# A hand-ordered pipeline drain: scatters in pairs, a fourth expert tile, other row buffers, and the second set of sums in parts

## The chip, the cores and the metric

The kernel runs on one core of a Trainium2 chip. The metric is device time in microseconds (us), the median of several runs. Beside it there is one profiled execution, with a time of its own, from which all durations below are taken.

## The reference, cut to what matters

Two layers work on an image of 2 x 256 x 56 x 56, that is 6272 tokens of 256 channels. The first layer (a convolution with neighbourhood attention) is not touched by the change. The second layer is this, per token:

```
t = t + attn(ln(t))      # linear attention, then a feed-forward of 512 units, each with a layer norm
#   Q = elu(q)+1, K = elu(k)+1;  KV = sum over an image's tokens of K*v;  msg = Q KV / (Q . sum K)
#   msg = layernorm(msg @ Wm);  h = relu([x, msg] @ W1) @ W2;  x + layernorm(h)
t = t + ffn(ln(t))       # 8 experts of 1024 units, the two best per token
#   probs = softmax(xt @ Wr);  top 2, weights normed to 1
#   y_e = gelu(layernorm(x) @ W1[e]) @ W2[e];  out = sum of weight * y_e over the two
```

All of it is float32. The two images have separate sums KV and K, so a second image's queries need its own sums.

## The kernel before, in words

**Groups and stages.** Layer 2 works on 49 blocks of 128 tokens, in 14 groups: eleven of four blocks, two of two, and one of one block (which holds the border of both images). A group is named below by its first block and its size, (45,2) for blocks 45 and 46. A group passes four stages, one step `s` of the main loop (L1777) apart: `queries` (letter q, two parts), `message` (m, two parts), `feed_forward` (f, four parts of the first matrix, then one for each two blocks of the second) and `route` (r, two parts, then p and P in the next step). Each of them is a generator. A part ends at a `yield`.

**The order.** TensorE's instructions are issued in the order in which they are traced (`manual_schedule`), and that order is written out by hand, as strings with a letter for each part: `turns` for the steps up to 11, `last` for steps 12 to 17. These last six steps are called the drain here: the queue of groups runs out, and expert tiles fill in. The other engines are ordered by the planner from its own priorities; `tc.issue_after(ins)` forces what is traced in its block to come behind `ins` on the same engine.

**Sums.** `merged(b, ...)` turns the key sums of image b into `ksm` and `mw`, in three rounds of matmuls with an eviction behind each. Image 1's runs at the end of step 5, behind `close_keys`, in one go.

**Route.** It normalises a group's rows into `row` (L147, on VectorE), whose columns 256 to 259 are the token number (copied from `dest` on GpSimd, L1710), two weights, and the better expert's number (copied on GpSimd, L1671). It transposes the rows (`pts`, L1486), multiplies by the router's weights (`pl`, L1719), picks two experts (`top_two`, a chain of some fifteen small VectorE instructions, with an Exp on ScalarE, L1657), and, after the part p with the matmuls `pp` (L1734 and L1735) on `chosen` (L1726), knows each row's place. Part P then writes every block's rows to DRAM (`xs`) with two indirect scatters per block on GpSimd (L160), all eight of a group in one part, behind the newest power of `route` (`power`). `row` has two buffers; a group of one block leaves the rest of its buffer to the next (`spare`).

**Powers.** Every inverse root is a power on GpSimd (`rs`, L254 and L1698). GpSimd also adds the residual (`t_b`, L1639), prepares an expert tile's output (`yt`, L1341) and scatters it with accumulation into `y` (L160 again).

**Expert tiles.** `Experts.run` takes tiles of 256 rows. One tile is 32 matmul instructions `ph` (L1359, four parts) with Gelu on ScalarE behind them (L1363), then `px` (L1332), the next tile's transposes, then 32 `py` (L1377, four parts). With a first part for the first transposes, three tiles are 25 parts: the letter e. `NFI` is the number of tiles that run in the drain; the others follow in a stage of their own (1407 to 2082 us) in which nothing else uses TensorE much.

**The end.** Tokens that received their last expert output late are read back, transposed (`pto`, L1866), evicted (`o_sb`, L1871 on ScalarE and L1873 on VectorE) and written out. `o_sb` comes from the pool `p4o`, which has four buffers.

Of the kernel before, what the change touches and what calls it, by code (L numbers as in the profile page):

```python
# [12 lines left out]
F32 = mybir.dt.float32  # L13
AF = mybir.ActivationFunctionType
ALU = mybir.AluOpType
# [4 lines left out]
P = 128  # L20
B, C, HH, WW = 2, 256, 56, 56
# [35 lines left out]
NFS, NHS = 48, 5  # L57
NFI = 3
XW = C + 4
# [59 lines left out]
def hybrid_kernel(ctx: ExitStack, tc: tile.TileContext, a: dict, out: bass.AP):  # L119
# [26 lines left out]
    def norm(out_, in_, mv, rstd, i):  # L146
        nc.vector.tensor_scalar(  # L147
            out_, in_, mv[:, i, 0:1], rstd[:, i : i + 1], ALU.subtract, ALU.mult
        )
# [16 lines left out]
    evac_n = [0]  # L166
    newest = [None]

# [80 lines left out]
    def rstd(sm, var, scale):  # L249
        n = var.shape[1]  # L250
        r = sm.tile([P, 4], F32, name="rs")
        with tc.high_priority():
            nc.vector.tensor_scalar(r[:, :n], var, scale, 1e-5, ALU.mult, ALU.add)  # L253
            nc.gpsimd.tensor_tensor(r[:, :n], r[:, :n], mhalf[:, :n], ALU.pow)  # L254
        return r
# [851 lines left out]
    class Experts:  # L1107
# [235 lines left out]
        def run(self, ts, pools, between=lambda i: None):  # L1343
# [7 lines left out]
            for i, (t, nh) in enumerate(ts):  # L1351
# [22 lines left out]
                for h in range(nh):  # L1374
                    py = pools.py(h)
                    for j in range(NJ):
                        nc.tensor.matmul(  # L1377
                            py, hT[:, j, h * P : (h + 1) * P], x.w2[:, j, :],
                            start=(j == 0), stop=(j == NJ - 1),
                        )  # L1380
                        if j == 3:
                            yield
                    newest[0] = nc.vector.scalar_tensor_tensor(  # L1383
                        x.yt[:, h, :], py, x.eq[:, h : h + 1], x.yt[:, h, :], ALU.mult, ALU.add
                    ).ins
                    scatter(y2, x.idi[:, h : h + 1], x.yt[:, h, :], mine, others, compute_op=ALU.add)
                    yield


    def layer1(ctx, tk, behind=(None, None)):  # L1390
# [19 lines left out]
        with lin as ph:  # L1410
# [86 lines left out]
            def merged(b, kxs, kc):  # L1497


                ksm = [wp.tile([P, P], F32, name=f"ksm{b}{hg}") for hg in range(2)]  # L1500
                mw = wp.tile([P, 2, C], F32, name=f"mw{b}")
                for hg in range(2):
                    nc.vector.tensor_scalar(ksm[hg], m32, kc[:, hg : hg + 1], None, ALU.mult)
                pt = ps_a.tile([P, 512], F32, name="kxt", tag="a")
                for ct in range(2):
                    for hg in range(2):
                        nc.tensor.transpose(
                            pt[:, (2 * ct + hg) * P : (2 * ct + hg + 1) * P],
                            kxs[:, hg, ct * P : (ct + 1) * P], ident,
                        )  # L1510
                kxt = wk.tile([P, 512], F32, name="kxt_sb", tag="tmp", bufs=4)
                evac(kxt, pt)
                kxt = kxt.rearrange("p (ct hg d) -> p ct hg d", ct=2, hg=2)
                pv = ps_a.tile([P, 512], F32, name="kvt", tag="a")
                kvt = wk.tile([P, 2, C], F32, name="kvt_sb", tag="u")[:, :, 0:P]
                for hg in range(2):
                    for ct in range(2):
                        nc.tensor.matmul(
                            pv[:, hg * P : (hg + 1) * P], w_v[:, ct, hg * P : (hg + 1) * P],
                            kxt[:, ct, hg, :], start=(ct == 0), stop=(ct == 1),  # L1520
                        )
                    nc.vector.tensor_tensor(kvt[:, hg, :], pv[:, hg * P : (hg + 1) * P], m32, ALU.mult)
                pm = ps_a.tile([P, 512], F32, name="mwp", tag="a")
                for hg in range(2):
                    nc.tensor.matmul(
                        pm[:, hg * C : (hg + 1) * C], kvt[:, hg, :], w_m[:, hg, :], start=True, stop=True
                    )
                evac(mw.rearrange("p hg c -> p (hg c)"), pm)
                centre(mw)
                return ksm, mw  # L1530

# [4 lines left out]
            def queries(n0, n, out):  # L1536
# [13 lines left out]
                for hg in range(2):  # L1550
                    pd = ps_q.tile([P, 512], F32, name="pd", tag="q")
                    for b, c0, c1 in parts(n0, n):
                        nc.tensor.matmul(
                            pd[:, c0:c1], sums[b][0][hg], qz[:, hg, c0:c1], start=True, stop=True
                        )
                    z = wk.tile([P, 512], F32, name="z")
                    over(z[:, :w], pd[:, :w], 1e-6)
# [48 lines left out]
            def feed_forward(n0, n, m2T):  # L1606
# [13 lines left out]
                for k0 in range(0, n, 2):  # L1620
# [26 lines left out]
            def top_two(lg, scale, row, n):  # L1647
# [32 lines left out]
                return ohs  # L1680


            spare = []
            power = [None]

            def route(n0, n):
# [3 lines left out]
                with tc.high_priority():  # L1690
# [12 lines left out]
                if n == 1:  # L1703
                    spare.append(row[:, 1:])
                row = row[:, :n]
                pts = [ps_a.tile([P, 512], F32, name="pts", tag="a") for _ in range(2)]
                for k in range(n):
                    norm(row[:, k, 0:C], t[:, k, :], mv, rs, k)
                    turn(pts, k, row[:, k, 0:C])
                nc.gpsimd.tensor_copy(row[:, :n, C], dest[:, n0 : n0 + n])  # L1710

# [33 lines left out]
                yield  # L1745

                with tc.issue_after(power[0]):
                    for k in range(n):
                        for kk in range(K):
# [3 lines left out]
                            )  # L1753
                yield

            sums[0] = merged(0, tk.kxs, tk.kc)
            kx = ps_k.tile([P, 2, C], F32, name="kx", tag="kx")
# [4 lines left out]
            for hg in range(2):  # L1764
# [5 lines left out]
            qzs, m2Ts = [], []  # L1770
            turns = "quvuvuqv", "mquvmuvquv", "mqfpPufmuqfurfvrfvfv"

            last = (
                "mqfpfmqfrfPrfef", "mqefpfemqfrePferf", "mfefpefmefrePfer", "fefpefefrePfer",
                "eeeeprePer", "eeeepP",
            )
            work = iter(())  # L1777
            tiles = iter(())


            with tc.manual_schedule(engines={mybir.EngineType.PE}):
                on = {}
                for s in range(ng + 4):
                    on = {"p": on.get("r", iter(()))}
                    if s < ng:
# [10 lines left out]
                    for part in turns[min(s, 2)] if s < ng - 2 else last[s - ng + 2]:  # L1796
                        next(tiles if part == "e" else on.get(part.lower(), iter(())), None)
                        chunk(work)
                        if part == "P" and s == early1 + 3:

                            tk.xa.close()
                            ex = Experts(ctx, tk)
                            pools = SimpleNamespace(
                                xr=lambda: wk.tile([P, 2, XW], F32, name="xr", tag="xt"),
                                xe=lambda: wk.tile([P, 2, ST], F32, name="xe", tag="ks"),
# [13 lines left out]
                            )  # L1819
                        if part == "P" and s == early2 + 3:  # L1820
                            ex.remember()
                    if s == 0:
                        prepare_feed_forward()
                    if s == 5:
                        kxs = wk.tile([P, 2, C], F32, name="kxs", tag="u")
                        kc = sm.tile([P, 2], F32, name="kc")
                        close_keys(tk, ps_a, kx, acc, kxs, kc)
                        sums[1] = merged(1, kxs, kc)
                for _ in tiles:
                    pass  # L1830

        with ExitStack() as ph:
# [7 lines left out]
            pools = SimpleNamespace(  # L1840
                xr=lambda: xp.tile([P, 2, XW], F32, name="xr"),
                xe=lambda: xp.tile([P, 2, ST], F32, name="xe"),
# [123 lines left out]
```

## Time and profile before

| what | us |
|---|---|
| median of the runs (lowest, highest) | 2113.43 (2113.14, 2123.83) |
| the profiled execution's own time | 2112.3 |
| its span, first to last instruction | 2110.5 |
| TensorE busy in the span | 1945.8 (92%) |
| VectorE, ScalarE, GpSimd busy | 1028.4, 633.4, 682.4 |
| steps 12 to 17, from the first `pm` of step 12 to the last `px` | 1246.9 to 1390.8 |
| one expert tile in its own stage | 14.26 (32 `ph` 6.91, `px` 0.44, 32 `py` 6.91) |
| TensorE busy from 2050 to 2110 | 37.7 of 60 |

The chain of work that ended last goes through TensorE for most of the second layer, so an interval in which TensorE has nothing to do there is an interval of the kernel's time. The granted clock in the profile says how much of TensorE's full speed was given in a stretch.

### The profile page before, as it was taken

Reading aid. Unit: us, or ns where it says so; the run is one execution under the profiler, and the core shown is the slowest. Engines: PE = TensorE matmul, PEld = TensorE weight load, DVE = VectorE, ACT = ScalarE, POOL = GpSimd, SP = SyncE. Lnnn points to the kernel's source line nnn. Section 1 sums busy time; section 2 is a strip of 40 time slices with the busy share of each in tenths; the row PEclk is TensorE's granted clock in tenths of the full one; section 3 lists DMA queues with packets and bytes.
Section 4 is the critical chain, followed back from the end, with each engine's and each line's share of the span. In section 5 each row is a group of like instructions: output and inputs, shape, how many; then the busy total and the mean of one; then the engine's idle time right before and its main releaser. Section 6 shows DMA issues by size and latency. Waiting matters only on the chain. (4 is left out here: it accounts for less than half of the span.)

```text
span 2110.5 us, 27961 instructions
## 1 busy us (share of the span) xinstructions
PE 1945.8 (92%) x10102; PEld 1364.8 (65%) x10102; DVE 1028.4 (49%) x2615; ACT 633.4 (30%) x1258; POOL 682.4 (32%) x800
## 2 busy tenths in 40 slices
PE   5799989999988888999999999799999999999995
PEld 3454444554434555666665657688888888888885
DVE  6777868775986656455555554351111212112121
ACT  1233323332332331333323223222222222222332
POOL 4712012111003433345444444442333333233221
PEclk9999989999988998999999999899999999999997
DMA  5642422344243214000011142377666666766994
GB/s 132 155 110 69 150 76 66 95 125 113 67 120 102 38 47 124 1 18 34 33 48 46 49 138 75 94 212 218 191 194 193 199 194 187 207 190 187 289 287 145
DMA packets 189784, 264.67 MB, mean 125 GB/s; under 512 B 26294, under 2 KB 149508, under 8 KB 189390
## 3 DMA queue, kind: packets, MB, share of 16 engines
q1 hardware_dynamic: 163598, 221.96, 34.6%
q0 software_dynamic: 20576, 29.75, 7.4%
q10 hardware_dynamic: 5456, 11.00, 1.6%
q8 instruction: 84, 1.38, 0.3%
q14 instruction: 70, 0.57, 0.1%
HBM read 196.38 MB, written 70.55 MB: 126 GB/s over the span
## 5 line engine op out<-in xcount | busy, mean ns | idle before, releaser
L1359 PE MATMUL ph<-xe,w1e 128*128 128x256 f32 (+1 forms) x1696 | 363.8, 372 | 4.7 <-DVE qz L237 3.6
L1377 PE MATMUL py<-w2e,hT 128*128 128x256 f32 x1616 | 358.6, 379 | 0.0
L1363 ACT ACTIVATE hT<-ph,sv 128x256 f32<-128x256 f32 (+1 forms) x424 | 196.3, 464 | 506.3 <-PE ph L1359 503.4
L1359 PEld LDWEIGHTS ph<-xe,w1e 128*128 128x128 f32 x1696 | 312.3, 192 | 45.8 <-DVE qz L237 3.8
L1377 PEld LDWEIGHTS py<-w2e,hT 128*128 128x128 f32 x1616 | 302.6, 190 | 38.8
L534 DVE SCALAR_TENSOR_TENSOR yc<-ypad,w,yc 128x1120 f32<-128x1120 f32 x192 | 267.3, 1395 | 46.0 <-ACT yc L532 43.0
L160 POOL DMA_INDIRECT y<-yt,idi x101 | 161.1, 1595 | 224.1 <-DVE yt L1383 133.0
L521 PE MATMUL pc<-ypad,diag 128*128 128x448 f32 x432 | 176.6, 549 | 0.5 <-ACT ypad L515 0.5
L509 PE MATMUL py<-x_sb,wq 128*128 128x448 f32 (+1 forms) x384 | 156.5, 539 | 14.6 <-ACT yc L525 9.2
L570 ACT ACTIVATE p<-p 98x680 f32<-98x680 f32 (+5 forms) x120 | 111.8, 932 | 182.9 <-DVE p L565 177.1
L565 DVE TENSOR_TENSOR p<-s_ps,tab 98x340 f32<-98x340 f32 (+5 forms) x240 | 138.1, 602 | 57.8 <-PE s_ps L561 56.3
L1315 DVE CAST idi<-xr 128x2 int32<-128x2 f32 (+1 forms) x53 | 10.0, 189 | 297.6 <-DMA xr<-xs 295.8
L1383 DVE SCALAR_TENSOR_TENSOR yt<-py,eq,yt 128x256 f32<-128x256 f32 x101 | 48.8, 483 | 210.9 <-PE py L1377 210.9
L561 PE MATMUL s_ps<-qT,kT 32*98 32x170 f32 (+5 forms) x960 | 131.3, 407 | 17.8 <-DVE p L565 16.6
L561 PEld LDWEIGHTS s_ps<-qT,kT 32*98 32x98 f32 (+1 forms) x960 | 57.6, 172 | 106.2 <-DVE p L565 59.6
L521 PEld LDWEIGHTS pc<-ypad,diag 128*128 128x128 f32 x432 | 78.1, 189 | 71.7 <-issue 68.0
L498 POOL TENSOR_SCALAR diag<-ident,w 128x128 f32<-128x128 f32 x108 | 84.9, 804 | 116.3 <-PE pc L521 109.4
L509 PEld LDWEIGHTS py<-x_sb,wq 128*128 128x128 f32 x384 | 70.9, 198 | 77.9 <-issue 54.9
L1341 POOL TENSOR_SCALAR yt<-b2e,eq 128x256 f32<-128x256 f32 x101 | 47.7, 485 | 217.1 <-DMA b2e<-in_L_ffn_b 215.2
L160 POOL DMA_INDIRECT xs<-row,si x98 | 96.4, 984 | 64.3 <-DVE si L1743 31.1
L254 POOL TENSOR_TENSOR rs<-rs,mhalf 128x2 f32<-128x2 f32 (+2 forms) x89 | 66.5, 754 | 142.1 <-DVE rs L253 118.4
L1614 PE MATMUL p<-m2T,fw 128*128 128x512 f32 (+2 forms) x224 | 94.3, 544 | 0.0
(357 smaller groups left out, 2606.0 us busy)
## 6 DMA issues: line engine op xcount, KB each, us to landing
w1e<-in_L_ffn_W SPq DMA_DIRECT2D x53, 1024.0 KB
w2e<-in_L_ffn_W SPq DMA_DIRECT2D x53, 1024.0 KB
yd<-yc SPq DMA_DIRECT2D x24, 784.0 KB
ld<-yd SPq DMA_DIRECT2D x28, 448.0 KB
xr<-xs SPq DMA_DIRECT2D x48, 260.0 KB
b2e<-in_L_ffn_b SPq DMA_DIRECT2D x53, 128.0 KB
yr<-y SPq DMA_DIRECT2D x11, 512.0 KB
td<-t_i SPq DMA_DIRECT2D x24, 224.0 KB
```

The source lines that it names most:

```text
L160: ins = nc.gpsimd.indirect_dma_start(out=dst[:, :], out_offset=bass.IndirectOffsetOnAxis(ap=index, axis=0), in_=src, in_offset=None, **kw,)
L498: nc.gpsimd.tensor_scalar(diag[:, tap, :], ident, w2[:, oc, tap : tap + 1], 1.0, ALU.mult, ALU.mult)
L509: nc.tensor.matmul(py[:, :n, :], wq1[:, ct, oc * P : (oc + 1) * P], x_sb[:, ct, (q0 + g0) * WW : (q0 + g0 + n) * WW], start=(ct == 0), sto ...
L521: nc.tensor.matmul(pc, diag[:, tap, :], ypad[:, dy : dy + 8, dx : dx + WW], start=(tap == 0), stop=(tap == 8),)
L534: nc.vector.scalar_tensor_tensor(yc[:, 8:, :], src, w, yc[:, 8:, :], ALU.mult, ALU.add)
L561: nc.tensor.matmul(s_ps[:nk, j, :n].rearrange("p (i j) -> p i j", j=nj), kT[hs], q[hs], start=True, stop=True,)
L565: nc.vector.tensor_tensor(p[:nk, 2 * pr : 2 * pr + 2, :n].rearrange("p h (i j) -> p h i j", j=nj), s_ps[:nk, :, :n].rearrange("p h (i j) - ...
L570: nc.scalar.activation(p[:nk, :, :n], p[:nk, :, :n], AF.Exp)
L1359: nc.tensor.matmul(p1, x.w1[:, ct, j * P : (j + 1) * P], x.xe[:, ct, :], start=(ct == 0), stop=(ct == 1),)
L1363: nc.scalar.activation(hT[:, j, :], p1, AF.Gelu, bias=x.sv[:, 4 + j : 5 + j])
L1377: nc.tensor.matmul(py, hT[:, j, h * P : (h + 1) * P], x.w2[:, j, :], start=(j == 0), stop=(j == NJ - 1),)
L1614: nc.tensor.matmul(p1[:, :w], fw1[:, k, oc * P : (oc + 1) * P], rhs, start=(k == 0), stop=(k == 3))
```

## The change

- `NFI` goes from 3 to 4, so a fourth expert tile runs in the drain and one fewer in the stage behind it.
- The scatters of a group are one pair per part. In the late groups each pair is issued behind the newest instruction in `newest[1]`: the last traced power of `rstd` or `route`, or the last residual addition. Expert outputs in the drain are scattered behind the same (`pools.turn`).
- The strings of the drain are written anew, with 35 letters e instead of 25. The set-up of the experts is moved to a letter of its own, c.
- Groups of fewer than four blocks take their rows from the buffers of `z`, which are made slightly larger, in place of the shared `row`.
- The expert's number is reduced straight into the row, and the token numbers are copied on VectorE behind the last norm; both copies on GpSimd go.
- `merged` is a generator with three parts. Image 1's run as the letters w in step 6.
- `p4o` has ten buffers instead of four.

```diff
-NFI = 3
+NFI = 4
     def rstd(sm, var, scale):
-            nc.gpsimd.tensor_tensor(r[:, :n], r[:, :n], mhalf[:, :n], ALU.pow)
+            newest[1] = nc.gpsimd.tensor_tensor(r[:, :n], r[:, :n], mhalf[:, :n], ALU.pow).ins
     def run(self, ts, pools, between=lambda i: None):
-                    scatter(y2, x.idi[:, h : h + 1], x.yt[:, h, :], mine, others, compute_op=ALU.add)
+                    with pools.turn():
+                        scatter(y2, x.idi[:, h : h + 1], x.yt[:, h, :], mine, others, compute_op=ALU.add)
             def merged(b, kxs, kc):
                 evac(kxt, pt)
+                yield
 ...
                     nc.vector.tensor_tensor(kvt[:, hg, :], pv[:, hg * P : (hg + 1) * P], m32, ALU.mult)
+                yield
 ...
                 centre(mw)
-                return ksm, mw
+                yield
             def queries(n0, n, out):
-                    z = wk.tile([P, 512], F32, name="z")
+                    z = wk.tile([P, 2 * XW], F32, name="z", tag="z")[:, :512]
             def feed_forward(n0, n, m2T):
-                    nc.gpsimd.tensor_tensor(tt, tt, u[:, :kn, :], ALU.add)
+                    newest[1] = nc.gpsimd.tensor_tensor(tt, tt, u[:, :kn, :], ALU.add).ins
             def top_two(lg, scale, row, n):
-                    ix = sm.tile([P, 4], F32, name=f"ix{k}")[:, :n]
+                    ix = sm.tile([P, 4], F32, name="ix")[:, :n] if k else row[:, :n, C + 3]
-                    if k == 0:
-                        nc.gpsimd.tensor_copy(row[:, :n, C + 3], ix)
             def route(n0, n):
-                    power[0] = nc.gpsimd.tensor_tensor(rs2, u, mhalf[:, :n], ALU.pow).ins
+                    newest[1] = nc.gpsimd.tensor_tensor(rs2, u, mhalf[:, :n], ALU.pow).ins
-                row = spare.pop() if spare else wk.tile([P, 4, XW], F32, name="row")
+                if n == 4:
+                    row = wk.tile([P, 4, XW], F32, name="row")
+                else:
+                    row = wk.tile([P, 2, XW], F32, name="row2", tag="z")[:, :n]
-                nc.gpsimd.tensor_copy(row[:, :n, C], dest[:, n0 : n0 + n])
+                with tc.issue_after(last.ins):
+                    nc.vector.tensor_copy(row[:, :n, C], dest[:, n0 : n0 + n])
-                with tc.issue_after(power[0]):
-                    for k in range(n):
+                for k in range(n):
+                    with tc.issue_after(newest[1]) if late else nullcontext():
                         for kk in range(K):
                             scatter(
 ...
-                yield
+                    yield
-            turns = "quvuvuqv", "mquvmuvquv", "mqfpPufmuqfurfvrfvfv"
+            turns = "quvuvuqv", "mquvmuvquv", "mqfpPPPPcufmuqfurfvrfvfv", "mwqfwpPPPPfwmqfrfrff"
             last = (
-                "mqfpfmqfrfPrfef", "mqefpefmqfrePferf", "mfefpefmefrePfer", "fefpefefrePfer",
-                "eeeeprePer", "eeeepP",
+                "mqfpcfmfqrfPPfPrPfe", "mqfpfmfqePePrePfePref", "mfefpefmeferePPfePerPe",
+                "fefeepefeferePfePere", "eeeeperPePer", "eeeepP",
             )
+                    if s == 6:
+                        on["w"] = second
-                        sums[1] = merged(1, kxs, kc)
+                        second = merged(1, kxs, kc)
-            op = ph.enter_context(tc.tile_pool(name="p4o", bufs=4, reuse_waits="tile"))
+            op = ph.enter_context(tc.tile_pool(name="p4o", bufs=10, reuse_waits="tile"))
```

More of the change, by code (lines that the diff above doesn't have):

```diff
@@ L146, in norm @@
     def norm(out_, in_, mv, rstd, i):
-        nc.vector.tensor_scalar(
+        return nc.vector.tensor_scalar(
             out_, in_, mv[:, i, 0:1], rstd[:, i : i + 1], ALU.subtract, ALU.mult
@@ L166, in hybrid_kernel @@
     evac_n = [0]
-    newest = [None]
+    newest = [None, None]
     def evac(dst, src):
@@ L1501, in merged @@
                 mw = wp.tile([P, 2, C], F32, name=f"mw{b}")
+                sums[b] = ksm, mw
                 for hg in range(2):
@@ L1680, in top_two @@
                 return ohs
-            spare = []
-            power = [None]
             def route(n0, n):
@@ L1701, in route @@
                 nc.vector.tensor_tensor(rs, rs, rs2, ALU.mult)
-                row = spare.pop() if spare else wk.tile([P, 4, XW], F32, name="row")
-                if n == 1:
-                    spare.append(row[:, 1:])
-                row = row[:, :n]
+                if n == 4:
+                    row = wk.tile([P, 4, XW], F32, name="row")
+                else:
+                    row = wk.tile([P, 2, XW], F32, name="row2", tag="z")[:, :n]
                 pts = [ps_a.tile([P, 512], F32, name="pts", tag="a") for _ in range(2)]
                 for k in range(n):
-                    norm(row[:, k, 0:C], t[:, k, :], mv, rs, k)
+                    last = norm(row[:, k, 0:C], t[:, k, :], mv, rs, k)
                     turn(pts, k, row[:, k, 0:C])
-                nc.gpsimd.tensor_copy(row[:, :n, C], dest[:, n0 : n0 + n])
+                with tc.issue_after(last.ins):
+                    nc.vector.tensor_copy(row[:, :n, C], dest[:, n0 : n0 + n])
                 x2T = tk.turned(n0, n)
@@ L1753, in route @@
                             )
-                yield
-            sums[0] = merged(0, tk.kxs, tk.kc)
+                    yield
+            for _ in merged(0, tk.kxs, tk.kc):
+                pass
             kx = ps_k.tile([P, 2, C], F32, name="kx", tag="kx")
@@ L1770, in layer1 @@
             qzs, m2Ts = [], []
-            turns = "quvuvuqv", "mquvmuvquv", "mqfpPufmuqfurfvrfvfv"
+            turns = "quvuvuqv", "mquvmuvquv", "mqfpPPPPcufmuqfurfvrfvfv", "mwqfwpPPPPfwmqfrfrff"
             last = (
-                "mqfpfmqfrfPrfef", "mqefpfemqfrePferf", "mfefpefmefrePfer", "fefpefefrePfer",
-                "eeeeprePer", "eeeepP",
+                "mqfpcfmfqrfPPfPrPfe", "mqfpfmfqePePrePfePref", "mfefpefmeferePPfePerPe",
+                "fefeepefeferePfePere", "eeeeperPePer", "eeeepP",
             )
             work = iter(())
-            tiles = iter(())
+            tiles = none = iter(())
             with tc.manual_schedule(engines={mybir.EngineType.PE}):
@@ L1783, in layer1 @@
                 for s in range(ng + 4):
-                    on = {"p": on.get("r", iter(()))}
+                    on = {"p": on.get("r", none)}
+                    if s == 6:
+                        on["w"] = second
                     if s < ng:
@@ L1795, in layer1 @@
                             on["uv"[k]] = keys(tk, wk, sm, ps_a, 4, kx, acc, groups[7 + s][0] + 2 * k, 2)
-                    for part in turns[min(s, 2)] if s < ng - 2 else last[s - ng + 2]:
-                        next(tiles if part == "e" else on.get(part.lower(), iter(())), None)
+                    for part in turns[3 if s == 6 else min(s, 2)] if s < ng - 2 else last[s - ng + 2]:
+                        next(tiles if part == "e" else on.get(part.lower(), none), None)
                         chunk(work)
-                        if part == "P" and s == early1 + 3:
+                        if part == "c" and s == early1 + 3:
                             tk.xa.close()
@@ L1803, in layer1 @@
                             pools = SimpleNamespace(
+                                turn=lambda: tc.issue_after(newest[1]),
                                 xr=lambda: wk.tile([P, 2, XW], F32, name="xr", tag="xt"),
@@ L1819, in layer1 @@
                             )
-                        if part == "P" and s == early2 + 3:
+                        if part == "c" and s == early2 + 3:
                             ex.remember()
@@ L1840, in layer1 @@
             pools = SimpleNamespace(
+                turn=nullcontext,
                 xr=lambda: xp.tile([P, 2, XW], F32, name="xr"),
```

## Prediction

> **What bounds it now.** I read the page first. TensorE is busy 92% of the span and fills the expert stage from 1407 to 2082 us, so only the holes outside that stage can be had. The 40 slices show two that this change can reach: slice 26 (1319 to 1372 us, busy 7, clock 8) and slice 40, the end. The weak slices 1 to 16 belong mostly to the first layer.
>
> ```profile
> PE 1945.8 (92%) x10102; PEld 1364.8 (65%) x10102; DVE 1028.4 (49%) x2615; ACT 633.4 (30%) x1258; POOL 682.4 (32%) x800
> PE   5799989999988888999999999799999999999995
> PEclk9999989999988998999999999899999999999997
> ```
>
> Then TensorE's waits from 1247 to 1400 us, which is the drain (columns: total us, times, longest):
>
> ```profile
> PE pp L1734 <- DVE chosen L1726: 13.4, 2, 12.0
> PE ph L1359 <- DVE qz L237: 3.6, 1, 3.6
> PE pd L1553 <- DVE m2T L175: 3.2, 1, 3.2
> ```
>
> These three lines are 20.2 us; with six small waits (3.2 us together) TensorE stands still 23.4 us. The stage table by windows adds the second price, a slow clock after the hole (columns: window, length, busy us of PE, PEld, DVE, ACT, POOL, clock, DMA share, GB/s):
>
> ```profile
> 1339.40:1351.40 12.00, 0.03 (x1) 0.00 (x0) 6.90 (x35) 2.85 (x6) 6.27 (x9) 0.70 0.24 56
> 1351.40:1358.00 6.60, 6.57 (x22) 5.79 (x23) 1.26 (x11) 1.14 (x3) 3.03 (x3) 0.51 0.11 40
> 1031.00:1040.00 9.00, 5.93 (x22) 4.76 (x22) 4.39 (x13) 0.78 (x2) 1.26 (x1) 0.65 0.09 31
> ```
>
> Why the 12 us? The timeline of GpSimd and VectorE at that place:
>
> ```profile
> 1334.41 0.17 DVE L253 TENSOR_SCALAR rs<-ssf 128x2 f32<-128x2 f32 x1 [3.35 <-ACT sq L1481]
> 1335.75 0.96 POOL L160 DMA_INDIRECT xs<-row,si  x1 [0.30 <-issue]
> 1339.34 0.18 POOL L1710 COPY row<-dest 128x2 f32<-128x2 f32 x1 [2.63 <-DMA xs<-row,si]
> 1340.01 1.60 POOL L160 DMA_INDIRECT y<-yt,idi  x1 [0.48 <-issue]
> 1341.04 1.33 POOL L254 TENSOR_TENSOR rs<-rs,mhalf 128x2 f32<-128x2 f32 x1
> 1342.40 0.88 DVE L1635 SCALAR_TENSOR_TENSOR u<-py,rs,g 128x256 f32<-128x256 f32 x2 [7.82 <-POOL rs L254]
> ```
>
> A power was wanted at 1334.6. GpSimd was in the midst of eight scatters (1.26 us each with the issue), then stood 2.6 us before the token-number copy, whose row buffer was still being read by the scatters, then scattered an expert output, and began the power at 1341.04. VectorE stood behind `u` with the router's chain of (45,2) queued after it, so `chosen` came at 1351.4, while TensorE had been given only 3.7 us of other work between `pl` and `pp`.
>
> **What the Trainium skill says.** "Advanced Engine Details and Errata", Sequencer Loop: an instruction waits in its engine's queue for its semaphores; the trace agrees, `u` and all behind it stood 7.8 us. "TensorE: Matmul & The Clock Gate", What's actually happening: an idle window of about 3.4 us halves the clock; the trace agrees after the 12 us (0.51), and shows slower matmuls after 3.2 us and 1.4 us too. "ScalarE: Activation LUTs", What ACT_TABLE_LOAD costs: 1283 ns per load; the drain has nine, mean 1283 ns. "DMA: Bandwidth & Descriptors", Anatomy of one DMA — SWDGE (gpsimd) path: about 2 us fixed; here a scatter of `row` lands after 2.5 us (median).
>
> **The change, part by part.** Warm, an 8-instruction part with 256 columns takes 1.73 us, with 512 columns 3.44; these price every letter.
>
> 1. *Pairs, rows elsewhere, copies off GpSimd, more e between `pl` and `pp`.* A power now finds at most one or two pairs (2.5 us each) and an output scatter (1.9) in front, not eight scatters. (45,2) no longer shares its buffer with groups whose scatters are under way; the two buffers of `z` are free by then, as the last queries end in step 13. Between the two parts of (45,2) the string had f e f, 3.7 us; it now has e f e f e e, 4 x 1.73 + 2 x 0.87 = 8.7 us. The undisturbed chain from `pl` to `chosen` is 3.9 us for (37,4) and 5.1 for (24,1), so it is covered. Gain: the wait of 12.0 and the slow clock (pp 1.04 for 0.22, ph 3.60 for 1.73, p 1.71 for 0.89: 3.5), **15.5**.
> 2. *An f between m and q in step 12.* `pd` waited for the m2T eviction, queued in VectorE behind four norms and the index chain until 1262.2. 3.44 us of f now run first. Gain 3.2 + slow clock (2.05 for 0.87, 4.21 for 3.44: 2.0) = **5.2**.
> 3. *The first e of step 13 behind q's second part.* `ph` waited 3.6 us for a buffer of `pq`, plus 0.7 slow. Now an f runs there. But e directly follows `pd`, whose two buffers are freed by transposes that ended 0.7 us after TensorE: I take 1.0 lost. Gain **3.3**.
> 4. *(47,2) in step 16:* five e instead of four before `pp`: 8.7 us of cover, where `pl` to `chosen` took 8.4. The 1.4 wait and 1.7 slow clock go: **3.1**.
> 5. *(24,1):* 33 parts e exist for 4 tiles, and the string uses two of them after the last `pl`: 3.5 us of cover where the chain takes 5.1, against four e (6.9) before. **-2.0** with its slow clock.
> 6. *The fourth tile* is 64 matmuls and `px` in both places: 14.3 us more in the drain, 14.26 less behind it, nothing net. Its four SP loads (0.38 us to issue each), two `yt` (0.47), one `so`, two output scatters on GpSimd and eight Gelus go along. SP's y writes and the weights have room: DMA is 0.2 to 0.4 busy there, and a tile now has 20 us or more for 2.2 MB that arrive in 14 in the later stage. If that cover failed, TensorE would wait for weights.
> 7. *New waits.* The trace of before cannot show the new order of GpSimd and VectorE. Every pair is now behind a power or a residual addition, and an output scatter too; queued behind them are the next powers and `yt`, for which VectorE waits. From below 0 (the orders fit; no gain, since an order is only added), from above a second wait like the old one, 12 with its clock 15. I take two waits of one pair, **-5**.
> 8. *Copies.* 28 GpSimd copies of 0.2 us go, 14 VectorE copies of under 0.2 come, right behind the norm that already holds the buffer. Both engines are under 60% busy: 0.
> 9. *Sums in parts.* At 1034 `kvt` waits for an eviction that sits behind statistics in VectorE, and the clock falls to 0.65:
>
> ```profile
> PE kvt L1518 <- DVE kxt_sb L175: 2.7, 1, 2.7
> ```
>
> Idle 3.1 and about 2 of slow clock. The parts w now have q and f (7 us) between; the short wait between the halves of `kvt` (0.4) stays. I take **3.5** of 5.1; from below 2.
>
> 10. *Ten buffers at the end.* From 2094 us the evictions wait for output transfers:
>
> ```profile
> DVE o_sb L1873 <- DMA out<-o_sb: 3.7, 3, 1.9
> ACT o_sb L1871 <- DMA out<-o_sb: 1.9, 2, 1.0
> ```
>
> The last group writes ten `o_sb`, so none waits. VectorE's 3.7 lie on the chain that ends last; the transfers then crowd a little. **3.0**, between 1 and 4. Twelve KB more of pool shift the later pools; what they land on is done with by 1390, so 0, at worst a couple of us.
>
> Sum: 15.5 + 5.2 + 3.3 + 3.1 - 2.0 - 5 + 3.5 + 3.0 = 26.6. The profiled execution took 2112.3 us, so 2085.7; it lies 1.1 under the median shown, so 2086.8. I say **2087**.
>
> **Rivals.**
> - *GpSimd's wait only moves.* Two pairs of (41,4) still stand ahead of `u`'s power of (47,2) in step 14, 5 us, with an output scatter 7, as long as before; then only the added cover of 5 us counts. Part 1 gives 5, parts 2 to 4 half of 11.6, less 5 and 2; with 6.5 from 9 and 10 that is 10: about 2102. For it: everything hangs on one queue that is half busy (25 of 50 us). Against: the missing 2.6 us buffer wait.
> - *ScalarE becomes the wait, and it is slower.* ScalarE takes Exp in order, ahead of Gelus, and before it stood up to 7.3 us at one Exp. `ph` has two buffers, 1.73 us of slack. Were each of five routes' Exp to fall among `ph`, TensorE would lose 2 x 1.28 + w - 1.73 each, w being the wait for VectorE. My sum without new waits gains 31.6; five such losses outweigh it from w = 5.5 us. At w = 7.3, the old longest, they cost 41, and five restarts with a cold clock 2 each (part 2's): 2112.3 - 31.6 + 51, about 2131. Against: counted by letters, each `pl` of steps 13 to 15 is followed by parts of `py`, which need no Gelu.
> - *It does not do what it says.* The planner may place pairs as before, late in a bunch; then only parts 9, 10 and the letters act, with the fourth tile's extra load: 2105 to 2115.
>
> **Chances.** Half a per cent, 10.6 us, is about what can be told from no change. My forecast 0.60 (2077 to 2098), the moved wait 0.22 (2098 to 2112, two thirds of it faster), no effect 0.08, ScalarE 0.10. So faster 0.74, same 0.14, slower 0.12. The range is 2077 (nothing in part 7, upper ends of 9 and 10) to 2112, which leaves out about 0.05 below and 0.15 above.
>
> **What would show it.** Right: no wait of TensorE over 3 us in the drain; `pp` waiting under 2; the longest run of scatters without a power two pairs; no GpSimd `row` copies; `kvt` waiting under 1; no `o_sb` waiting for `out`; the drain, from the first `pm` of step 12 to the `px` behind the last `pp`, some 138 us (144 + 14 - 20), though it holds one tile more; the stage behind it 14 us shorter. Wrong: a wait of 5 us or more at `pp`, `ph` or `u`, `ph` waiting for a Gelu, or a clock under 0.9 between 1300 and 1400.

## The result and the profile after

The changed kernel takes **2087.22 us** (median of six runs, 2085.41 to 2098.08); the kernel before, beside it, 2112.61 (six runs, 2102.24 to 2123.83). The ratio is 0.9889, with a 95% interval of 0.9853 to 0.9925. The forecast was 2087, in a range from 2077 to 2112. The number came out; the steps behind it did so only in part.

The profiled execution took 2085.57 us. From its page: the span, the busy time by engine, and two rows of the 40 slices.

```profile
span 2083.8 us, 27912 instructions
PE 1931.9 (93%) x10102; PEld 1354.2 (65%) x10102; DVE 1024.8 (49%) x2629; ACT 633.0 (30%) x1258; POOL 676.2 (32%) x772
PE   5799989999988888999999998999999999999996
PEclk9999989999997998999999999999999999999998
```

Slice 26, which stood at 7 with a clock of 8, is full; slice 25 has gone from 9 to 8, for new waits that are shown below. TensorE has the same 10102 matmul instructions; GpSimd has 28 fewer, the copies. TensorE's waits in the drain of the changed kernel (engine, operation and line, what it waited for, total us, times, longest):

```profile
PE pp L1734 <- DVE chosen L1726: 3.9, 2, 2.3
PE ph L1360 <- ACT hT L1364: 2.2, 3, 1.0
PE pp L1735 <- DVE before L1731: 2.2, 1, 2.2
PE pp L1734 <- DVE oh L1672: 2.0, 1, 2.0
```

The waits of 12.0, 3.6 and 3.2 us are gone. The longest left is 2.3.

Because one profile's total can mislead, I cut every profile at the same five instructions: the first `pm` of steps 5, 7 and 12, the `px` of the 40th expert tile before the end, and the last `py`. Counting that tile from the end makes the work of "drain" equal, whatever `NFI` is. Lengths in us:

| kernel | to step 5 | 5, 6 (sums) | 7 to 11 | drain | stage | end |
|---|---|---|---|---|---|---|
| before | 988.1 | 85.8 | 173.0 | 281.6 | 553.7 | 28.4 |
| after | 984.1 | 81.0 | 173.4 | 266.4 | 554.9 | 23.9 |

The drain gives 15.2, the sums 4.8, the end 4.5. The 3.9 us ahead of step 5 are not the change's: they are there when layer 2 begins (its first `pq` starts at 801.7 before and at 797.1 after), and the first layer is the same. Over all profiles of this study the stretch to step 5 lies between 979.0 and 991.9. It alone makes totals spread by half a per cent, so the experiments below are read by their stretches first. (In the diff of the change one old string is misprinted; step 13 of the kernel before reads `mqefpfemqfrePferf`.)

### The profile page after: what moved, and what is told of

The parts are those of the page before. It is cut to its first block, busy times and chain, and to the rows that moved or that the text cites. A ratio compares the mean times of both kernels' runs of the same rounds, so it can differ in the third digit from the quotient of the medians.

```text
span 2083.8 us, 27912 instructions
## 1 busy us (share of the span) xinstructions
PE 1931.9 (93%) x10102; PEld 1354.2 (65%) x10102; DVE 1024.8 (49%) x2629; ACT 633.0 (30%) x1258; POOL 676.2 (32%) x772
## 4 chain that ended last, share of the span: by engine, by line
PE 62%; DVE 15%; POOL 5%; DMA 5%; ACT 4%; issue 3%; SPq 0%; DVEq 0%; ACTq 0%; POOLq 0%
PE ph L1360 16%; PE py L1378 15%; PE p L1619 5%; PE py L510 4%; PE po L575 4%; PE pc L522 4%; DVE yc L535 3%; PE s_ps L562 3%; DVE p L566 2%; POOL rs L255 2%; DMA y<-yt,idi 2%; PE kx L299 2%; PE s_ps L359 2%; PE kp L286 1%; PE py L1631 1%
## 5 line engine op out<-in xcount | busy, mean ns | idle before, releaser
L1316 DVE CAST idi<-xr 128x2 int32<-128x2 f32 (+1 forms) x53 | 10.4, 196 | 304.1 <-DMA xr<-xs 299.2
```

## The experiments

The theory was the prediction's: one queue. Eight scatters in one part made a power late, and pairs put behind powers cured it. The rival: the letters did it, since they give TensorE more to do while the chain runs, and the pairs bring little.

**The letters alone, e2.** The kernel before with the new strings of the drain and four tiles (the set-up of the experts goes to its letter c with them). The scatters stay in one part of eight, the rows in the shared buffers, the copies on GpSimd, the sums in one go, `p4o` at four.

```diff
-NFI = 3
+NFI = 4
 ...
-                "mqfpfmfqrfPrfef", "mqefpfemqfrePferf", "mfefpefmefrePfer", "fefpefefrePfer",
-                "eeeeprePer", "eeeepP",
+                "mqfpcfmfqrfPPfPrPfe", "mqfpfmfqePePrePfePref", "mfefpefmeferePPfePerPe",
+                "fefeepefeferePfePere", "eeeeperPePer", "eeeepP",
 ...
```

> The kernel before with the new strings of the drain and four tiles only; scatters in one part, shared rows, copies on GpSimd, sums and four output buffers as before. Theory GpSimd: the waits for m2T and qz go, the 12 us at pp shrink by the cover of 5 us to some 6, drain 272 to 279. Rival letters: drain 265 to 268. If the old wait stays whole, 280.

Measured: 2097.52 us, ratio 0.9914 (0.9885 to 0.9942); sums 85.4, **drain 266.6**, end 28.5. The whole gain of the drain is there without a single pair: the letters and the fourth tile that they need are enough. To see why, follow one chain: the power is asked for when VectorE has written `rs` (L253), then come the power, `u`, and at last `chosen`, for which `pp` of (45,2) waits. VectorE in the kernel with the letters alone (start, length, engine, line; in brackets the idle time before and what ended it):

```profile
1335.43 0.17 DVE L253 TENSOR_SCALAR rs<-ssf 128x2 f32<-128x2 f32 x1 [3.98 <-ACT sq L1481]
1336.51 0.88 DVE L1635 SCALAR_TENSOR_TENSOR u<-py,rs,g 128x256 f32<-128x256 f32 x2 [0.91 <-POOL rs L254]
1347.11 0.16 DVE L1726 TENSOR_TENSOR chosen<-oh,oh 128x16 f32<-128x16 f32 x1
```

and GpSimd at that place:

```profile
1330.52 0.96 POOL L160 DMA_INDIRECT xs<-row,si  x1 [0.30 <-issue]
1331.79 1.60 POOL L160 DMA_INDIRECT y<-yt,idi  x1 [0.30 <-DVE idi L1315]
1333.96 0.18 POOL L1710 COPY row<-dest 128x2 f32<-128x2 f32 x1 [0.58 <-issue]
1335.75 0.72 POOL L254 TENSOR_TENSOR rs<-rs,mhalf 128x2 f32<-128x2 f32 x1 [0.69 <-DVE rs L253]
```

From asking to `chosen` it takes 11.7 us (1335.60 to 1347.27), and TensorE has work until 1347.62, so `pp` follows without a wait:

```profile
1344.17 3.62 PE L1377 MATMUL py<-w2e,hT 128*128 128x256 f32 x16
1347.62 0.29 PE L1734 MATMUL pp<-chosen,tri 128*128 128x16 f32 x2
```

The last of the eight scatters ended at 1331.5, and the copy behind them waited 0.6. Now the same sum for the kernel before:

```profile
1338.82 0.61 PE L1614 MATMUL p<-m2T,fw 128*128 128x128 f32 x4
1351.20 0.17 DVE L1726 TENSOR_TENSOR chosen<-oh,oh 128x16 f32<-128x16 f32 x1
1351.43 0.61 PE L1734 MATMUL pp<-chosen,tri 128*128 128x16 f32 x2 [12.00 <-DVE chosen L1726]
```

With the lines that the prediction shows: asked at 1334.58, `u` at 1342.40, `chosen` done at 1351.37, so 7.8 and then 9.0 us. TensorE's last work ahead of `pp` ended at 1339.43, 4.85 us after the asking. 7.8 + 9.0 - 4.85 = 12.0, the wait. By this sum, had the power come at once (`u` 0.9 after the asking, as in e2), some 5 us of wait would have been left, for want of work. That is an estimate: no run has the pairs under the old letters. The letters mended both: TensorE has 12 us of work from the asking on, and the scatters begin 3.2 us earlier while the power is asked for 1.0 later (these two drains start within 0.1 us of each other, so the times compare as they stand).

**The pairs undone, e1.** The changed kernel with all scatters of a group in the first P.

```diff
-                for k in range(n):
-                    with tc.issue_after(newest[1]) if late else nullcontext():
+                with tc.issue_after(newest[1]) if late else nullcontext():
+                    for k in range(n):
 ...
-                    yield
+                yield
```

> The changed kernel, but a group's scatters are again one part, all behind one power; letters, fourth tile, rows and copies stay changed. The drain is measured from the first pm of step 12 to the px of the 40th tile from the end: 281.6 us before, 266.4 after. Theory GpSimd (a power behind eight scatters makes the long wait): a wait of TensorE at pp or at pd comes back, 4 us or more, and the drain takes 272 to 280. Rival letters (the added cover alone does it): 265 to 268, no wait over 3 us.

Measured: 2088.64 us, ratio 0.9898 (0.9845 to 0.9952); **drain 265.1**, where the changed kernel has 266.4. So the pairs are not what shortens the drain. VectorE, and `pp` on TensorE, in the kernel with one part, and then in the changed kernel:

```profile
1319.43 0.17 DVE L254 TENSOR_SCALAR rs<-ssf 128x2 f32<-128x2 f32 x1 [3.62 <-ACT sq L1483]
1320.50 0.87 DVE L1640 SCALAR_TENSOR_TENSOR u<-py,rs,g 128x256 f32<-128x256 f32 x2 [0.90 <-POOL rs L255]
1324.80 0.34 DVE L1693 TENSOR_TENSOR u<-mv,rs 128x2 f32<-128x2 f32 x1 [0.64 <-POOL rs L255]
1330.73 0.17 DVE L1726 TENSOR_TENSOR chosen<-oh,oh 128x16 f32<-128x16 f32 x1
1331.62 0.29 PE L1734 MATMUL pp<-chosen,tri 128*128 128x16 f32 x2
```

```profile
1326.00 0.17 DVE L254 TENSOR_SCALAR rs<-ssf 128x2 f32<-128x2 f32 x1 [2.67 <-ACT sq L1483]
1327.07 0.88 DVE L1640 SCALAR_TENSOR_TENSOR u<-py,rs,g 128x256 f32<-128x256 f32 x2 [0.90 <-POOL rs L255]
1333.86 0.16 DVE L1693 TENSOR_TENSOR u<-mv,rs 128x2 f32<-128x2 f32 x1 [2.60 <-POOL rs L255]
1339.66 0.16 DVE L1726 TENSOR_TENSOR chosen<-oh,oh 128x16 f32<-128x16 f32 x1
1339.97 0.37 PE L1734 MATMUL pp<-chosen,tri 128*128 128x16 f32 x2 [1.61 <-DVE chosen L1726]
```

In both `u` waits 0.9 for its power. From `u` to the end of `chosen` the one part takes 10.4 us, the pairs 12.75: pairs stand in front of the route's own power, for which VectorE waits 2.60 in place of 0.64. In the changed kernel `pp` of (45,2) waits 1.6 for that, with one part it doesn't. The same happens at (37,4), where the power for `u` came behind two pairs of (33,4). The timeline of GpSimd, VectorE and TensorE in the changed kernel there:

```profile
1271.58 0.97 POOL L160 DMA_INDIRECT xs<-row,si  x1 [0.30 <-issue]
1272.85 0.96 POOL L160 DMA_INDIRECT xs<-row,si  x1 [0.30 <-issue]
1273.84 0.72 POOL L255 TENSOR_TENSOR rs<-rs,mhalf 128x2 f32<-128x2 f32 x1
...
1274.60 0.48 DVE L1640 SCALAR_TENSOR_TENSOR u<-py,rs,g 128x256 f32<-128x256 f32 x1 [2.65 <-POOL rs L255]
1275.00 0.18 DVE L1726 TENSOR_TENSOR chosen<-oh,oh 128x32 f32<-128x32 f32 x1
...
1275.32 0.38 PE L1734 MATMUL pp<-chosen,tri 128*128 128x32 f32 x2 [2.33 <-DVE chosen L1726]
1277.89 0.43 PE L1735 MATMUL pp<-before,ones 128*128 128x32 f32 x2 [2.18 <-DVE before L1731]
```

The power began the moment the last scatter ended, `u` stood 2.65, `chosen` was queued behind it. With one part this wait of 2.33 is 0.59. The 2.18 behind it is in both, so the pairs don't make it.

**No forced order, e7.** The changed kernel with pairs and output scatters wherever the planner likes them.

```diff
-                    with tc.issue_after(newest[1]) if late else nullcontext():
+                    with nullcontext():
 ...
-                                turn=lambda: tc.issue_after(newest[1]),
+                                turn=nullcontext,
```

> The changed kernel with the scatters in pairs, but no pair and no expert output forced behind a power or an addition. Theory: the planner puts pairs ahead of some powers again; one or two waits of 2 to 5 us, drain 268 to 274. Rival: the parts' places in the strings are enough, drain 265 to 268.

Measured: 2081.31 us, ratio 0.9868 (0.9838 to 0.9898); drain 262.9. On every engine its instructions stand in the same order as those of e1: left to itself the planner puts the pairs together again. So e1 and e7 are two measurements of one program. They show the order without the pairs at 265.1 and 262.9, and how far one program's drain varies from profile to profile.

**The changed kernel again, e13**, without an edit, for the same reason.

> The changed kernel once more, to see how far two profiles of one program differ. One part and no forced order turned out to be the same instruction orders, with drains of 265.1 and 262.9. If that is the size of the variation, this drain lies within 264 to 269, and pairs against one part (266.4) are not told apart by one profile.

Measured: 2089.39 us, ratio 0.9893 (0.9869 to 0.9918); drain 268.3, with the waits of 2.33, 2.18 and 1.62 at the same places. The means are 267.3 with pairs and 264.0 without, 3.3 apart, which is about the pairs' two waits (2.33 - 0.59 or nothing, and 1.61). The waits are plain; that the total is worse with pairs isn't settled by two profiles each, with ratios whose intervals overlap. One thing that makes the same program differ can be seen. In the first profile the clock was 0.50 from 1220.12 to 1223.53, in step 11, and in e13 it was not, at the same short waits; in e13 it was 0.50 for as long behind the 1.62 at `pp`, and in the first profile, behind 1.61, it was not. Each time costs some 1.7 us, once ahead of the cut at step 12 and once behind it: from step 7 to the end of the drain the two take 439.8 and 440.0 us.

**Twice the burst, e11 and e12.** Is the queue harmless, then? Every row of (41,4) is scattered a second time, into a buffer that nobody reads, in e11 on top of e1 (16 scatters in one part), in e12 on top of the changed kernel (four parts of four).

```diff
 ...
                             scatter(xs, ...)
+                            if n0 == 41:
+                                scatter(xs2, si[:, kk, k : k + 1], row[:, k, :], [f"xd{run}"], [f"xd{run}"])
```

> The changed kernel with scatters in one part, and with each of the eight scatters of (41,4) done twice, the second time into a buffer that nothing reads: 10.1 us more on GpSimd ahead of the power that the old kernel waited for. The one-part kernel had 4.0 us between the end of the burst with its expert output and the start of that power. Theory queue with slack (the letters gave the burst room, no more): the power starts some 6 us late, and pp of (45,2) waits 5 us or more. Rival (TensorE's cover alone decides): pp waits under 3.

> The changed kernel, pairs as they are, with the same eight extra scatters of (41,4). Theory: two pairs come before the power, two behind, so at most half of the extra time is ahead of it, and pp of (45,2) waits 2 to 5 us, less than with one part. Rival (pairs never matter): the same wait as with one part.

Measured: e11 2096.68 us, ratio 0.9926 (0.9903 to 0.9949), drain 275.0; e12 2093.0, ratio 0.9908 (0.9877 to 0.9939), drain 271.5. The timeline of GpSimd and TensorE in e11, the one part:

```profile
1333.85 0.96 POOL L161 DMA_INDIRECT xs<-row,si  x1 [0.30 <-issue]
...
1335.74 0.72 POOL L256 TENSOR_TENSOR rs<-rs,mhalf 128x2 f32<-128x2 f32 x1
...
1337.43 6.72 PE L1379 MATMUL py<-w2e,hT 128*128 128x256 f32 x16 [2.96 <-DVE u L1641]
1347.04 0.58 PE L1735 MATMUL pp<-chosen,tri 128*128 128x16 f32 x2 [2.89 <-DVE chosen L1727]
```

Here the queue bites: `u` stood 10.7 us, TensorE waited twice, and 16 `py` took 6.72 where they take 3.46 (two parts of 1.73) at full clock. The drain is 10 us over e1's. Counted from each drain's start, the power began 7.7 us later than in e1 (95.8 against 88.1). The eight extra scatters are 10.1 us (8 x 1.26); 1.5 of them went into the time for which e1's GpSimd stood idle ahead of that power, about one into small shifts. In e12:

```profile
1327.21 0.72 POOL L256 TENSOR_TENSOR rs<-rs,mhalf 128x2 f32<-128x2 f32 x1 [0.22 <-DVE rs L255]
...
1344.56 0.58 PE L1735 MATMUL pp<-chosen,tri 128*128 128x16 f32 x2 [5.31 <-DVE chosen L1727]
```

The pairs do keep the first power on time, but the chain from `u` to `chosen` stretches to 16.4 us and `pp` waits 5.3. The sizes were given only roughly beforehand: e12's 5.3 lies above what was expected, and e11's loss came as two waits and a slow clock, not as one wait. By their drains, one profile each, the pairs are worth 3.5 us against one part when the burst is twice as long; in this kernel, where the burst fits in front of the power, no gain from them is seen.

**Three tiles, e6.** The changed kernel with `NFI = 3` under the new strings.

```diff
-NFI = 4
+NFI = 3
```

> The changed kernel with three expert tiles in the drain; the letters are the same, those past 25 find nothing. Theory cover (the fourth tile's parts cover the last routes): pp of (47,2) and (24,1) and the last rows wait, drain 270 to 280. Rival: the fourth tile is only moved, drain 266 to 268.

Measured: 2097.12 us, ratio 0.9939 (0.9913 to 0.9966); drain 274.8, which is 7.5 over the mean of the changed kernel's two. With one tile less there is too little expert work for the last letters, and TensorE stands at two `pp`:

```profile
1360.18 0.61 PE L1734 MATMUL pp<-chosen,tri 128*128 128x16 f32 x2 [4.06 <-DVE chosen L1726]
1366.42 0.59 PE L1734 MATMUL pp<-chosen,tri 128*128 128x8 f32 x2 [3.50 <-DVE chosen L1726]
```

So the fourth tile, no gain as work, is worth 7 to 8 us as cover for the chains of (47,2) and (24,1). That is nearly half of what the drain gains: the new order of the letters alone would not have given all of it.

**The rows and the copies, e3 and e4.** The changed kernel with the small groups' rows in the shared buffers again (e3), or with both copies on GpSimd again (e4).

```diff
 ...
+                row = spare.pop() if spare else wk.tile([P, 4, XW], F32, name="row")
 ...
```

```diff
 ...
+                        nc.gpsimd.tensor_copy(row[:, :n, C + 3], ix)
 ...
+                nc.gpsimd.tensor_copy(row[:, :n, C], dest[:, n0 : n0 + n])
```

> The changed kernel with the shared row buffers of before. Theory GpSimd: the buffer wait of 2.6 us now stands on VectorE in front of a norm, at most 2 to 3 us are lost, drain 266 to 269. Rival rows (the buffer wait was the head of the long wait): VectorE stands for the rows' transfer with the router's chain behind it, a wait of 5 us or more, drain 271 or more.

> The changed kernel with both copies back on GpSimd. Theory GpSimd queue: copies of 0.2 us wait for VectorE in GpSimd's queue, but what is behind them is not late: drain 266 to 268. Rival: a copy that waits for VectorE holds up powers, drain 270 or more.

Measured: e3 2090.71 us, ratio 0.9894 (0.9857 to 0.9931), drain 269.9; e4 2092.72, ratio 0.9888 (0.9851 to 0.9925), drain 268.8. In each, the `pp` with the longest wait waits 2.5 us. Both drains lie about 1 us above what was expected (1.3 us of e3's is a wait of `ph` in the expert tiles behind the last route, where the changed kernel has 0.6 and none). Against 266.4 and 268.3 for the changed kernel neither can be told from nothing; at most they are worth two or three us.

**The sums and the end alone, e5.** The kernel before with `merged` in three parts, w in step 6, and ten buffers in `p4o`.

```diff
 ...
-            turns = "quvuvuqv", "mquvmuvquv", "mqfpPufmuqfurfvrfvfv"
+            turns = "quvuvuqv", "mquvmuvquv", "mqfpPufmuqfurfvrfvfv", "mwqfwpPfwmqfrfrff"
 ...
-            op = ph.enter_context(tc.tile_pool(name="p4o", bufs=4, reuse_waits="tile"))
+            op = ph.enter_context(tc.tile_pool(name="p4o", bufs=10, reuse_waits="tile"))
```

> The kernel before with two parts of the change that lie outside the drain: the second sums in parts, and ten output buffers. Measured by stages: from the first pm of step 5 to that of step 7 (85.8 us before, 81.0 after) 81 if the parts alone do it; from the last py to the end (28.4 before, 23.9 after) 24 if the buffers do it; the drain stays at 281 to 282. Rival: the gains between the two profiles are the chip's variation, then 85 and 28.

Measured: 2108.38 us (20 runs), ratio 0.9986 (0.9974 to 0.9998); sums 81.1, drain **285.7**, end 24.8. By their stretches the two parts bring 4.7 and 3.6 us, but the kernel became only 2 to 3 faster. In its profile the drain was 4.2 longer than in the one of before (steps 7 to 11 were 1.6 shorter, 171.4 against 173.0). The old wait was there, and longer:

```profile
1337.27 0.19 POOL L1713 COPY row<-dest 128x2 f32<-128x2 f32 x1 [4.17 <-DMA xs<-row,si]
...
1349.37 0.61 PE L1737 MATMUL pp<-chosen,tri 128*128 128x16 f32 x2 [13.56 <-DVE chosen L1729]
```

The copy's wait for the rows' transfer is 4.17 here and was 2.63: GpSimd has the same order of instructions in both, but the last scatter of the burst landed 4.8 us after its issue, before 3.2. Whether that is variation of the old, fragile order or something that the earlier sums bring about, one profile on each side doesn't tell; it stays open. In the changed kernel no copy waits there.

**A fifth tile, e8 and e14.** e8 is the changed kernel with `NFI = 5`. e14 is e7 with `NFI = 5` and one f of step 13 ahead of p, not behind it.

```diff
-NFI = 4
+NFI = 5
```

```diff
-                "mqfpcfmfqrfPPfPrPfe", "mqfpfmfqePePrePfePref", "mfefpefmeferePPfePerPe",
+                "mqfpcfmfqrfPPfPrPfe", "mqffpmfqePePrePfePref", "mfefpefmeferePPfePerPe",
```

> The changed kernel with five tiles in the drain, so that the four parts in front of the last pp are real. Theory: the wait of 2.0 us at the last pp and the slow clock behind it (16 ph in 5.4 instead of 3.5) go, drain 262 to 264. Rival: that wait only moves to the next transposes, drain 266.

> The changed kernel without forced order, with five tiles in the drain, and the part p of step 13 one f later. Theory cover: the waits at pp of (37,4) (2.2) and of (24,1) (2.0 with a slow clock of 2) go, drain 257 to 261, total 4 us under the changed kernel. Rival: the waits move on, drain 262 to 266, total as before.

Measured: e8 2089.38 us, ratio 0.9894 (0.9864 to 0.9925), drain 266.8; e14 **2084.2**, ratio 0.9856 (0.9829 to 0.9883), drain 261.8. TensorE's two longest groups of waits in e14's drain:

```profile
PE ph L1360 <- ACT hT L1364: 2.3, 3, 1.0
PE pd L1558 <- DVE m2T L176: 1.4, 1, 1.4
```

In e14's drain no `pp` waits any more, and no wait is over 1.4 us. e8 shows that the last `pp` waits no more with a fifth tile, while the pairs' waits stay; its drain is no shorter, against what was expected. e14 has the lowest ratio, and its median is 5 us under that of e13 (2089.39) on the same chip; the two ratios' intervals overlap a little, so that it beats the changed kernel is likely, not settled. From e7, 0.9868, it isn't told apart.

## Why the prediction was right, and where it was not

**The sum.** Predicted: drain 20.1, sums 3.5, end 3.0, together 26.6. Measured by the stretches, as means of the profiles with and without each part: drain 16.3 (281.6 and 285.7 against 266.4 and 268.3), sums 4.6 (85.6 against 81.0), end 3.7 (28.44 against a mean of 24.77), together 24.6, and 25.4 by the medians. The forecast was met because a drain over-sized by 3.8 stood beside two small parts under-sized by 1.8, and because the sum was set against a profile whose time is a chance of half a per cent. That it came within a microsecond is luck.

**Step 1, the size right and the cause wrong.** The wait of 12.0 went and most of the slow clock with it. But it was put down to the pairs, the rows and the copies, with the letters as an addition ("so it is covered"). e2 and e1 show the reverse: the letters with the fourth tile do it alone, where the first rival gave added cover 5 of the 15.5 us, and undoing the pairs loses nothing. The error was to take the delay seen in front of the power for the wait. 7.8 of the chain's 16.8 us were in front of `u`; even without the scatters, by the sum above, the cover of 4.85 fell 5 us short. And the "undisturbed chain from `pl` to `chosen`" of 3.9 to 5.1 us was the wrong piece to cover: `chosen` stood behind `u`, so the chain begins at the power's asking and is 11 to 12 us long.

**Steps 2, 3 and 4** hold: the waits of `pd` (3.2), of `ph` for `qz` (3.6) and of `pp` of (47,2) (1.4) are gone. The 1.0 that step 3 set aside for a wait behind `pd` was not lost, so it gave 4.3.

**Step 5** was under-sized: -2.0, measured about -3.9. TensorE of the changed kernel at (24,1):

```profile
1378.14 0.39 PE L1734 MATMUL pp<-chosen,tri 128*128 128x8 f32 x2 [1.96 <-DVE oh L1672]
...
1380.17 5.41 PE L1360 MATMUL ph<-xe,w1e 128*128 128x256 f32 x16 [0.93 <-DVE xe L1336]
```

The wait is 1.96, and behind it 16 `ph` take 5.41 where they take 3.46.

**Step 6** holds as work: from the first `pm` of step 12 to the `px` behind the last `pp` is 140.0 us (1238.57 to 1378.60), where 138 was given. That the tile is also the cover which the letters need, 7 to 8 us, was not in the sum; e6 showed it.

**Step 7**, new waits, -5, measured -7.9: 2.33 and 1.61 from pairs, as described, 2.18 from a place that has nothing to do with them, and 1.8 of slow clock, since the eight `p` behind take 3.50 us (from 1278.13 to 1281.63) where the next eight take 1.73. With steps 3, 5 and 7 as measured, steps 1 to 7 give 15.5 + 5.2 + 4.3 + 3.1 - 3.9 - 7.9 = 16.3; with the 2.2 us for which `ph` now waits for Gelus, which the sum left out, 14.1. Measured are 15.2 in the pair of profiles and 16.3 by the means.

**Step 8**, 0: e4 can't be told from it. **Step 9**, 3.5: measured 4.6. The wait of 2.7 is gone and with it the slow clock; the short one, between the halves of `kvt`, has grown from 0.4 to 1.39, so the sign "under 1" was wrong:

```profile
1039.91 0.71 PE L1522 MATMUL kvt<-kxt_sb,w_v 128*128 128x128 f32 x4 [1.39 <-DVE kvt_sb L1526]
```

**Step 10**, 3.0: measured 3.7. Of the evictions that waited for output transfers (3.7 on VectorE, 1.9 on ScalarE) this is left in the changed kernel:

```profile
ACT o_sb L1875 <- DMA out<-o_sb: 0.7, 1, 0.7
```

**The rivals.** *The wait only moves* is half true: new waits came, but of 2.3 and 1.6 us, not the 5 to 7 that would give 2102. *ScalarE becomes the wait*: `ph` waits for a Gelu 2.2 us in three places, none over 1.0, where five losses of over 6 us were needed (2 x 1.28 + 5.5 - 1.73). *It does not do what it says*: the ratio excludes no effect. What this rival feared, pairs in a bunch, is what e7 has, and it costs nothing there. Faster, to which 0.74 was given, is what came.

**The signs.** Of those for "right" these failed: "`pp` waiting under 2" (2.33), "the longest run of scatters without a power two pairs" (step 13 has four pairs back to back, from 1281.86 to 1291.75), `kvt` under 1, and no `o_sb` waiting. Of those for "wrong" two came, in small: `ph` waits for Gelus, and the clock is 0.83 from 1378 to 1388.

## What to carry to other kernels

Where an engine waits for a chain, add up the whole chain from the first instruction that was asked for too late, and set it against the work that the waiting engine has from that same moment: here 7.8 + 9.0 - 4.85 = 12.0. The sum says how much a shorter queue can give and how much only more work in between can give; here it leaves 5 us to more work alone. Splitting a burst on a shared queue helped the first in line here and held up the ones behind (0.9 us before the first `u`, 16.4 from there to `chosen` in e12), so ask first whether the burst is longer than the slack in front of it; and when runs of one program differ by more than the change, cut the profiles at fixed instructions and compare stretches.

## What was not expected of the hardware

- Matmuls ran slow after short waits. The Trainium skill, "TensorE: Matmul & The Clock Gate", What's actually happening, speaks of an idle window of about 3.4 us; here 16 `ph` took 5.41 us for 3.46 after waits of 1.96 and 0.93, and e11's `py` 6.72 for 3.46 after 2.96. The record of the granted clock shows more of it. In the second layer the clock is 0.50 for stretches of 3.41 us or whole multiples, and in one profile their starts lie whole multiples of 3.413 us apart (from 1220.12 in the changed kernel 17, 47 and 247 of them). A slow stretch that is filled with matmuls loses 1.7 us; in the drain they add about a third to the waits (some 8 to 23.4 us before, 3.4 to 11.8 after).
- What counted was how long TensorE stood still within one such stretch. With time cut at those multiples, from step 7 to the end of the drain in all fourteen profiles, a slow stretch followed every full-speed one in which TensorE stood still 1.9 us or more in sum (27 of 27), and none with less than 1.3; in between it followed 13 of 23. The ends of matmuls are modelled in the trace, so these limits are rough. A gap's place counts too: the 1.62 us at e13's `pp` lie within one stretch, and the clock fell; the 1.61 of the first profile are split into 1.23 and 0.38, and it did not.
- The stretch to step 5 took 979.0 to 991.9 us over the profiles of the study, while the sums took 81.0 to 81.1 wherever they were in parts. Most of that spread is there when layer 2 begins (793.7 to 804.5 us).
